# One division step for the first two head pairs: the softmax sums of layer 1 taken together

## The chip, the cores and the metric

The kernel runs as one launch on one core of a Trainium2 chip. The metric is the device time of that launch in microseconds (us); a kernel's time is the median over several executions. Before the change it is 3047.86 us, the median of 3 runs from 3046.55 to 3050.51.

## The reference, cut to what matters

Eight images of 384 channels and 32 x 32 pixels, that is 1024 tokens of 384 channels, pass through two layers in fp32. Layer 0 (group norm, attention with a relative bias, a residual) isn't touched. Layer 1 does the following, and the change is in its attention, whose softmax is divided only after the product with v:

```
t = to_tokens(x)
t = t + attention(layer_norm(t))       # 6 heads of 64; q and k normalised over each head
t = t + feed_forward(layer_norm(t))    # images 0 to 4 only; the reference leaves the output
                                       # of the last three images at zero there
attention:
    attn = softmax(einsum('bhnd,bhmd->bhnm', q, k) * scale, axis=-1)
    out  = einsum('bhnm,bhmd->bhnd', attn, v)
    return out @ proj_w.T + proj_b
```

## The kernel before, in words

Layer 1 works on one image after the other. The six heads of an image are three **pairs** (0, 1 and 2): the two heads of a pair, j = 0 and 1, lie in the two halves of the 128 partitions. The 1024 queries are two halves (h, 512 each), and the 1024 keys are eight groups of 128, taken two at a time (m2 = 0 to 3). A **unit** is one (pair, h, m2), so an image has 24 units, numbered 0 to 23 here: pair 0 is units 0 to 7, pair 1 is 8 to 15, pair 2 is 16 to 23.

The loop over units is written out by hand, and every engine gets its instructions in the order of the text:

- `scores` (L1322) makes the scores s of a unit on TensorE in two PSUM tiles; ScalarE takes the exponential of them into two SBUF tiles e (L1333). VectorE adds the e tiles of a half into running sums t (L1345 for the first two, L1348 after). At m2 = 3 it adds the two halves of t into one half of a tile `folded[pair, j]`, named f in the profile (L1353).
- `weigh` (L1371) multiplies e with v into the PSUM tile o. It runs two units behind `scores` (LAG = 2), between the scores of its step and those of the next one. When a half is finished, ScalarE and VectorE bring o into `oT` (L1380, L1381).
- `divide` is called once for each pair, when the last unit of the pair has been weighed: for pair 0 in step 9 of the loop, for pair 1 in step 17, for pair 2 after the loop. Four matmuls with a column of ones (L1394, tile sum) give the sums over partitions for (j, h), each in its own group of 32 PSUM partitions. ScalarE copies them out (L1399, tile sr), SyncE's queue sends them to DRAM (L1408, sd) and fetches them again spread over 128 partitions (L1409, inv). VectorE takes the reciprocal (L1412), SyncE's queue writes it to DRAM (L1414, rd) and fetches it twice broadcast over 64 partitions (L1417, rb). VectorE multiplies `oT[:, pair]` by rb (L1419).

The waiting parts of `divide` are put off with `later.after(n, work)`: the work is placed n steps of the loop later, so that its instructions stand behind those of the units in between.

Buffers set part of the order. PSUM has four tiles of two banks (`mm2`), shared by s, o, sum and everything else. SBUF has a pool of 16 tiles of 128 x 1024 (`wtile`), which e, t, f, sr and the squares of the next image share. rb has one buffer. At step 3 of an image the next image is loaded, and its sums and squares (L1109, L1122, L1128, L1132) are placed at steps 13, 14, 15, 19 and 20.

After the loop, images 0 to 4 run the output projection (`project_out`, L1435) and the feed-forward; images 5 and 6 run the next image's q, k and v, with the projection put into the next image's loop; image 7 finishes with pair 2's division and the projection.

```
if done and done[0][1:] == (NH - 1, MT // 2 - 1):
    divide(b, oT, done[0][0])
later.step()
```

Of the kernel before, what the change touches and what calls it, by code (L numbers as in the profile page):

```python
# [19 lines left out]
F32 = mybir.dt.float32  # L20
# [7 lines left out]
P = 128  # L28
QP = P // 2
B, C, IH, IW = 8, 384, 32, 32  # L30
N = IH * IW
KC = C // P
MT = N // P
HALF = 512
NH = N // HALF
# [16 lines left out]
H1, D1 = 6, 64  # L52
NP1 = H1 // 2
# [43 lines left out]
class _Shared:  # L97
# [13 lines left out]
    def mm2(self, name):  # L111
        return self.ps.tile([P, NH, HALF], F32, tag="p", name=name)
# [918 lines left out]
def _layer1(tc, ins, x1, out, shared, start, before=None, check=None):  # L1031
# [3 lines left out]
    nc = tc.nc  # L1035
    with ExitStack() as ctx:

        def pool(name, bufs):
            return ctx.enter_context(tc.tile_pool(name=name, bufs=bufs, reuse_waits="tile"))
# [5 lines left out]
        small = pool("b_small", 2)  # L1045
        dram = ctx.enter_context(tc.tile_pool(name="b_dram", bufs=2, space=DRAM))
        later = _Later()
        mm2 = shared.mm2
        rsqrt, ones = shared.rsqrt, shared.ones

        def wtile(name, shape=(P, N)):
            return work.tile(list(shape), F32, tag="w", name=name)

        def flat2(t):
            return t.rearrange("p h q -> p (h q)")
# [253 lines left out]
        acc, total, folded = {}, {}, {}  # L1309
# [75 lines left out]
            for finish in weigh(b, oT, *done) or ():  # L1385
                finish()

        def divide(b, oT, pair, steps=(2, 2)):


            pst = mm2(f"sum{b}_{pair}")
            for h in range(NH):
                for j in range(2):
                    nc.tensor.matmul(  # L1394
                        pst[ts(2 * j + h, 32), 0], ones[:, 0:32], folded[pair, j][:, ts(h, HALF)],
                        start=True, stop=True,
                    )
            rows = wtile(f"sr{b}_{pair}", (P, HALF))
            nc.scalar.copy(rows, pst[:, 0])  # L1399
            sd = dram.tile([4, HALF], F32, tag="sd", name=f"sd{b}_{pair}")  # L1400
            rd = dram.tile([2, N], F32, tag="rd", name=f"rd{b}_{pair}")
            inv = small.tile([P, 2 * N // P], F32, tag="inv", name=f"inv{b}_{pair}")

            def spread(t):
                return t.rearrange("a q -> (a q)").rearrange("(p c) -> p c", p=P)

            with nc.allow_non_contiguous_dma(reason="sums"):
                nc.sync.dma_start(sd, rows[0:P:32])  # L1408
                nc.sync.dma_start(inv, spread(sd))  # L1409

            def invert():
                nc.vector.reciprocal(inv, inv)  # L1412
                with nc.allow_non_contiguous_dma(reason="sums"):
                    nc.sync.dma_start(spread(rd), inv)  # L1414
                rb = room.tile([P, N], F32, tag="rb", name=f"rb{b}_{pair}")
                for j in range(2):
                    nc.sync.dma_start(rb[ts(j, D1)], rd[j].partition_broadcast(D1))  # L1417
                later.after(
                    steps[1], lambda: nc.vector.tensor_mul(oT[:, pair], oT[:, pair], rb)  # L1419
                )  # L1420

            later.after(steps[0], invert)

# [187 lines left out]
        def head_rows(b):  # L1611
            return dram.tile([NP1, 8, HALF], F32, tag="hs", name=f"hd{b}")
# [49 lines left out]
        for b in range(B):  # L1662


            assert B // NG == 1
            ffn, more = b < NG, b + 1 < B
            oT = None
            if b == 1 and check is not None:
                for i, stage in enumerate(check(wtile)):
                    later.after(2 * i + 5, stage)  # L1670
            held = []
            for i, u in enumerate(units):
                done = held.pop(0) if len(held) == LAG else None
                held.append(
                    (u, scores(b, qk, kc, u, lambda: weigh(b, oT, *done) if done else None))
                )
                if done and done[0][1:] == (NH - 1, MT // 2 - 1):
                    divide(b, oT, done[0][0])
                later.step()
                if i == 3:  # L1680
                    if behind is not None:
                        behind()
                        behind = None
                    oT = wide.tile([P, KC, N], F32, tag="o", name=f"oT{b}")
                    ahead = load(b + 1) if more else None
                    if more:
                        *ahead_sums, stages = fold(f"a{b + 1}", ahead)
                        for at, stage in zip((13, 14, 15, 19, 20), stages):
                            later.after(at - i, stage)
            if not more:  # L1690
                for done in held:
                    weigh_last(b, oT, done)
                divide(b, oT, NP1 - 1)
                later.finish()
                project_out(b, oT, xt, lambda m: store(b, xt, m))
                break
            if not ffn:

                def last(i, b=b, oT=oT, held=held):
                    weigh_last(b, oT, held[i])  # L1700
                    if i == 1:
                        divide(b, oT, NP1 - 1, (2, 4))

                nqk, nkc = attention_inputs(
                    b + 1, ahead, [lambda: last(0), lambda: last(1)], ahead_sums
                )
                behind = lambda b=b, oT=oT, xt=xt: project_out(
                    b, oT, xt, lambda m: store(b, xt, m)
                )
            else:  # L1710
                nqk, sq, d, nkc = {}, {}, head_rows(b + 1), kc_tile(b + 1)

                def project(pair, s, step=True, middle=None):
                    return project_qk(b + 1, pair, s, ahead, nqk, sq, step, middle)

                def normalise(pair, *steps):
                    normalise_qk(b + 1, pair, nqk, d, nkc, steps)

                for i in range(2):
                    project_v(b + 1, ahead, i)  # L1720
                    weigh_last(b, oT, held[i])
                divide(b, oT, NP1 - 1, (1, 1))
                project_v(b + 1, ahead, 2)
                fsq, fc = [], []
                project_out(b, oT, xt, lambda m: fsq.append(square(f"f{b}", xt, m)), later.step)
                two = wtile(f"two{b}")
                nc.vector.tensor_add(two, xt[:, 0], xt[:, 1])
                nc.vector.tensor_add(fsq[0], fsq[0], fsq[1])
                project(
                    0, 0,  # L1730
                    middle=lambda: fc.append(
                        token_sums(f"f{b}", (xt[:, KC - 1], two), (fsq[KC - 1], fsq[0]))
                    ),
                )
                un, begin, normal = layer_norm(b, xt, fc[0])
                tk = token_sums(f"a{b + 1}", *ahead_sums)
                project(0, 1)
                take = project(1, 0, step=False)
                begin()
                take()  # L1740
                later.step()
                head_sums(b + 1, 0, sq, d)
                take = project(1, 1, step=False)
                normal()
                take()

                def between_1(m):
                    if m == 2:
                        normalise(0, 5, 2)
                    elif m == 4:  # L1750
                        head_sums(b + 1, 1, sq, d)
                        normalise(1, 5, 3)

                y1, top = feed_forward_1(b, un, between_1)
                project(2, 0)
                quant_scale(top)
                supply = Supply(b, y1, top)
                supply.gelu(0)
                supply.gelu(1)
                supply.split(0)  # L1760
                project(2, 1, step=False)()
                supply.split(1)
                supply.gelu(2)
                project_v(b + 1, ahead, MT // 2 - 1, copy=nc.scalar.copy)

                def between_2(k):
                    if k == 0:
                        head_sums(b + 1, 2, sq, d)
                        normalise(2, 6, 3)
                    elif k == 4:  # L1770
                        token_stats(f"a{b + 1}", tk)
                    elif k > 4 and (k - 5) % 2 == 0:
                        scale_v(tk, (k - 5) // 2)

                feed_forward_2(b, supply, between_2, xt)
            xt, qk, kc = ahead, nqk, nkc
# [74 lines left out]
```

## Time and profile before

| | us |
|---|---|
| median of 3 runs | 3047.86 |
| the profiled execution's own time | 3046.46 |
| its span (first to last instruction) | 3044.7 |
| TensorE busy in the span | 3018.3 |
| VectorE busy | 1772.1 |
| ScalarE busy | 1401.9 |
| GpSimd busy | 465.1 |

The span is what the profile's times are counted in. The profiled execution took 1.76 us more than its span, and 1.40 us less than the median of the runs. A matmul with fp32 operands shows as two records. Ends of matmuls are modelled in the profile and overlap the next matmul's start, so distances on TensorE are read from start to start. "PEld" is TensorE's weight load, "SPq" is SyncE's queue, which issues the DMAs.

### The profile page before, as it was taken

The numbers are of one execution on the slowest core, as the hardware profiler recorded it, in microseconds if no ns is written. First come the engines' busy times: TensorE is split into PE (matmuls) and PEld (weight loads), VectorE is DVE, ScalarE is ACT, GpSimd is POOL, SyncE is SP. The second block draws the span as 40 slices with busy tenths as digits, with TensorE's granted clock in tenths as the row PEclk, the third lists the DMA queues.
The fourth block names the chain that finished last, engine by engine and source line by source line (L and its number), as shares of the span: only waits on it lengthen the run. The fifth ranks groups of instructions, "written<-read, shape, count | busy, mean of one in ns | idle before, by whom it ended". The sixth has DMA issues, their size and how long they took to land.

```text
span 3044.7 us, 45670 instructions
## 1 busy us (share of the span) xinstructions
PE 3018.3 (99%) x18914; PEld 1598.8 (53%) x18914; DVE 1772.1 (58%) x1768; ACT 1401.9 (46%) x1768; POOL 465.1 (15%) x315
## 2 busy tenths in 40 slices
PE   8999999999999999999999999999999999999998
PEld 3455546455554645444545645645645646645453
DVE  3746647373655727355565765765755755754555
ACT  2634526253443616244463553553553544654544
POOL 0111102021110202123202202202202202211110
PEclk9999999999999999999999999999999999999999
DMA  7412020211212020121401101101101101102011
GB/s 178 119 25 83 19 82 23 72 30 26 76 22 79 23 83 19 37 87 51 120 23 37 50 16 37 50 23 30 50 23 30 50 22 30 55 12 72 16 51 44
DMA packets 102769, 150.49 MB, mean 49 GB/s; under 512 B 62260, under 2 KB 65828, under 8 KB 101784
## 3 DMA queue, kind: packets, MB, share of 16 engines
q1 hardware_dynamic: 99688, 147.41, 17.2%
q8 instruction: 152, 2.49, 0.3%
q14 instruction: 65, 0.53, 0.1%
q10 hardware_dynamic: 2864, 0.05, 0.1%
HBM read 111.05 MB, written 27.32 MB: 45 GB/s over the span
## 4 chain that ended last, share of the span: by engine, by line
PE 96%; DMA 1%; DVE 1%; SPq 1%; issue 0%; ACT 0%; ACTq 0%; DVEq 0%
PE s L521 14%; PE o L552 14%; PE s L1322 11%; PE o L1371 11%; PE pq L1178 8%; PE pq L467 8%; PE y2p L1575 6%; PE y1p L1524 5%; PE pp L616 4%; PE pv L1259 4%; PE pp L1435 4%; PE pv L495 4%; PE sum L1394 1%; PE hs L1207 1%; SPq L391 1%; DMA wide<-table 0%
## 5 line engine op out<-in xcount | busy, mean ns | idle before, releaser
L536 ACT ACTIVATE e<-e 128x1024 f32<-128x1024 f32 x512 | 535.0, 1057 | 441.7 <-DVE e L532 421.8
L532 DVE TENSOR_TENSOR e<-s,grow 128x1024 f32<-128x1024 f32 x512 | 601.4, 1219 | 190.3 <-PE s L521 189.7
L521 PE MATMUL s<-qk 48*64 48x512 f32 x4096 | 611.1, 591 | 3.2 <-DVE e L532 3.1
L552 PE MATMUL o<-e,v 64*64 64x512 f32 x4096 | 607.4, 589 | 1.4 <-DVE e L532 1.4
L1333 ACT ACTIVATE e<-s,kc 128x512 f32<-128x512 f32 x768 | 463.4, 693 | 181.8 <-PE s L1322 165.2
L1322 PE MATMUL s<-qk,qk 64*64 64x512 f32 x3072 | 398.7, 592 | 1.3 <-DVE oT L1381 1.2
L1371 PE MATMUL o<-e,v 64*64 64x512 f32 x3072 | 395.6, 591 | 0.0
L521 PEld LDWEIGHTS s<-qk 48*64 48x64 f32 x4096 | 237.2, 132 | 228.5 <-issue 76.0
L552 PEld LDWEIGHTS o<-e,v 64*64 64x64 f32 x4096 | 259.7, 133 | 178.9 <-issue 72.0
L1348 DVE TENSOR_TENSOR t<-t,e 128x1024 f32<-128x1024 f32 x192 | 231.0, 1222 | 65.6 <-ACT e L1333 65.6
L1178 PE MATMUL pq<-bx,wqkv 128*128 128x512 f32 x576 | 255.4, 597 | 0.7 <-ACT tra L1150 0.7
L467 PE MATMUL pq<-xn,w 128*128 128x512 f32 x576 | 251.8, 598 | 0.0
L1322 PEld LDWEIGHTS s<-qk,qk 64*64 64x64 f32 x3072 | 148.9, 133 | 195.5 <-issue 116.3
L581 POOL TENSOR_TENSOR inv<-sums,over 128x16 f32<-128x16 f32 x32 | 92.7, 2898 | 1008.7 <-DMA sums<-sd 850.0
L1371 PEld LDWEIGHTS o<-e,v 64*64 64x64 f32 x3072 | 148.3, 133 | 180.5 <-issue 142.5
L467 PEld LDWEIGHTS pq<-xn,w 128*128 128x128 f32 x576 | 109.8, 192 | 142.7 <-issue 140.0
L1178 PEld LDWEIGHTS pq<-bx,wqkv 128*128 128x128 f32 x576 | 107.7, 190 | 145.0 <-issue 141.3
L1345 DVE TENSOR_TENSOR t<-e,e 128x1024 f32<-128x1024 f32 x96 | 114.2, 1224 | 58.5 <-ACT e L1333 58.3
L1511 DVE TENSOR_REDUCE parts<-y 128x1 f32<-128x1024 f32 x75 | 90.0, 1217 | 93.8 <-ACT y L1508 93.3
L1228 POOL TENSOR_TENSOR hc<-hc,rsqrt 128x32 f32<-128x32 f32 x24 | 140.1, 5836 | 2.0
L1194 ACT ACTIVATE qsq<-pq 128x1024 f32<-128x1024 f32 x48 | 49.1, 1024 | 194.1 <-DVE qk L1188 105.5
L477 DVE TENSOR_SCALAR qk<-pq,bqk 128x1024 f32<-128x1024 f32 x24 | 30.8, 1284 | 177.5 <-PE pq L467 177.5
(161 smaller groups left out, 3032.1 us busy)
## 6 DMA issues: line engine op xcount, KB each, us to landing
rb<-rd SPq DMA_DIRECT2D x112, 256.0 KB
xn<-in_x_dram SPq DMA_DIRECT2D x24, 512.0 KB
res<-in_x_dram SPq DMA_DIRECT2D x24, 512.0 KB
x<-res SPq DMA_DIRECT2D x24, 512.0 KB
bx<-x SPq DMA_DIRECT2D x8, 1536.0 KB
rq<-hi SPq DMA_DIRECT2D x48, 256.0 KB
out_dram<-bx SPq DMA_DIRECT2D x24, 512.0 KB
wide<-table SPq DMA_DIRECT2D x80, 114.2 KB
```

Source lines behind the costliest of these rows:

```text
L467: nc.tensor.matmul(pq[:, h], wqk[:, k, s, 2 * pair : 2 * pair + 2, :].rearrange("p h d -> p (h d)"), xn[:, k, ts(h, HALF)], start=(k == 0) ...
L521: nc.tensor.matmul(s[j][ts(c, QP), i], qk[pair][rows, 1, ts(4 * m2 + 2 * i + c, QP)], qk[pair][rows, 0, ts(h, HALF)], start=True, stop=True,)
L532: nc.vector.tensor_add(e.rearrange("p (i q) -> p i q", i=2), s[j], bass.AP(near.tensor, near.offset, [near.ap[0], [-QROWS * IW, 2], [1, HA ...
L536: nc.scalar.activation(e, e, AF.Exp)
L552: nc.tensor.matmul(po[ts(j, S0), r], v[keys, 2 * m2 + i, 2 * pair + j, :], es[j][keys, ts(i, HALF)], start=(m2 == 0 and i == 0), stop=(m2 ...
L1178: nc.tensor.matmul(pq[:, h], wqkv[:, k, s * C + pair * P : s * C + (pair + 1) * P], xt[:, k, ts(h, HALF)], start=(k == 0), stop=(k == KC - 1),
L1322: nc.tensor.matmul(s[j][ts(c, QP), i], qk[pair, 1][rows, ts(4 * m2 + 2 * i + c, QP)], qk[pair, 0][rows, ts(h, HALF)], start=True, stop=True,)
L1333: nc.scalar.activation(e[:, ts(i, HALF)], s[j][:, i], AF.Exp, scale=kc[:, pair, j, m : m + 1])
L1348: nc.vector.tensor_add(total[j], total[j], e)
L1371: nc.tensor.matmul(po[ts(j, D1), r], v[keys, 2 * m2 + i, at : at + D1], es[j][keys, ts(i, HALF)], start=(m2 == 0 and i == 0), stop=(m2 == ...
L1524: nc.tensor.matmul(py[m][:, h], w1[:, k, ts(m, P)], un[k][i][:, ts(h, HALF)], start=(k == 0 and i == 0), stop=(k == KC - 1 and i == 1),)
L1575: nc.tensor.matmul(py[m][:, h], w2[:, k, ts(m, P)], supply.parts[k][i][:, ts(h, HALF)], start=(k == 0 and i == 0), stop=(k == FC - 1 and i ...
```

## The change

`divide` takes a list of pairs. It is called once for the pairs 0 and 1, in step 17, where it stood for pair 1 before; pair 2 has a call of its own as before. For two pairs the sums are eight matmuls into both banks of one PSUM tile, the copy takes 128 x 1024 elements, sd, inv and rd hold twice as much, and there is one reciprocal. Each pair still has its own rb and multiplication: `use(0)` fetches rb for pair 0; two steps later pair 0 is multiplied and `use(1)` fetches rb for pair 1, which is multiplied two steps after that. So pair 0 is multiplied in step 20 (it was step 12) and pair 1 in step 22 (it was step 20). The tiles f of pair 0, first written in step 3, are held up to step 17 (they were free after step 9). Per image there are one copy, one reciprocal and three DMAs fewer.

```diff
-        def divide(b, oT, pair, steps=(2, 2)):
-            pst = mm2(f"sum{b}_{pair}")
-            for h in range(NH):
-                for j in range(2):
-                    nc.tensor.matmul(
-                        pst[ts(2 * j + h, 32), 0], ones[:, 0:32], folded[pair, j][:, ts(h, HALF)],
-                        start=True, stop=True,
-                    )
-            rows = wtile(f"sr{b}_{pair}", (P, HALF))
-            nc.scalar.copy(rows, pst[:, 0])
-            sd = dram.tile([4, HALF], F32, tag="sd", name=f"sd{b}_{pair}")
-            rd = dram.tile([2, N], F32, tag="rd", name=f"rd{b}_{pair}")
-            inv = small.tile([P, 2 * N // P], F32, tag="inv", name=f"inv{b}_{pair}")
+        def divide(b, oT, pairs, steps=(2, 2)):
+            n = len(pairs)
+            name = f"{b}_{pairs[0]}"
+            pst = mm2(f"sum{name}")
+            for i, pair in enumerate(pairs):
+                for h in range(NH):
+                    for j in range(2):
+                        nc.tensor.matmul(
+                            pst[ts(2 * j + h, 32), i], ones[:, 0:32],
+                            folded[pair, j][:, ts(h, HALF)], start=True, stop=True,
+                        )
+            rows = wtile(f"sr{name}", (P, n * HALF))
+            nc.scalar.copy(rows, flat2(pst[:, 0:n]))
+            sd = dram.tile([4, n * HALF], F32, tag=f"sd{n}", name=f"sd{name}")
+            rd = dram.tile([4, n * HALF], F32, tag=f"rd{n}", name=f"rd{name}")
+            inv = small.tile([P, n * 2 * N // P], F32, tag=f"inv{n}", name=f"inv{name}")
...
                     nc.sync.dma_start(spread(rd), inv)
+                use(0)
+
+            def use(i):
+                pair = pairs[i]
                 rb = room.tile([P, N], F32, tag="rb", name=f"rb{b}_{pair}")
                 for j in range(2):
-                    nc.sync.dma_start(rb[ts(j, D1)], rd[j].partition_broadcast(D1))
-                later.after(
-                    steps[1], lambda: nc.vector.tensor_mul(oT[:, pair], oT[:, pair], rb)
-                )
+                    nc.sync.dma_start(
+                        rb[ts(j, D1)].rearrange("p (h q) -> p h q", h=NH),
+                        bass.AP(
+                            rd.tensor, rd.offset + (2 * j * n + i) * HALF,
+                            [[0, D1], [n * HALF, NH], [1, HALF]],
+                        ),
+                    )
+
+                def multiply():
+                    nc.vector.tensor_mul(oT[:, pair], oT[:, pair], rb)
+                    if i + 1 < n:
+                        use(i + 1)
+
+                later.after(steps[1], multiply)
...
-                if done and done[0][1:] == (NH - 1, MT // 2 - 1):
-                    divide(b, oT, done[0][0])
+                if done and done[0] == (NP1 - 2, NH - 1, MT // 2 - 1):
+                    divide(b, oT, range(NP1 - 1))
```

The three other calls pass `[NP1 - 1]` for `NP1 - 1`.

More of the change, by code (lines that the diff above doesn't have):

```diff
@@ L1692, in _layer1 @@
                     weigh_last(b, oT, done)
-                divide(b, oT, NP1 - 1)
+                divide(b, oT, [NP1 - 1])
                 later.finish()
@@ L1701, in last @@
                     if i == 1:
-                        divide(b, oT, NP1 - 1, (2, 4))
+                        divide(b, oT, [NP1 - 1], (2, 4))
                 nqk, nkc = attention_inputs(
@@ L1721, in _layer1 @@
                     weigh_last(b, oT, held[i])
-                divide(b, oT, NP1 - 1, (1, 1))
+                divide(b, oT, [NP1 - 1], (1, 1))
                 project_v(b + 1, ahead, 2)
```

## The prediction

> **What bounds the kernel now.** I read the page's busy times first, then its chain of work, then TensorE's instructions in order of time around one of the steps that the change touches (image 2, pair 1), then VectorE's.
>
> ```profile
> PE 3018.3 (99%) x18914; PEld 1598.8 (53%) x18914; DVE 1772.1 (58%) x1768; ACT 1401.9 (46%) x1768; POOL 465.1 (15%) x315
> ...
> PE 96%; DMA 1%; DVE 1%; SPq 1%; issue 0%; ACT 0%; ACTq 0%; DVEq 0%
> ```
>
> TensorE is busy 99% of the span and is 96% of the chain. Only what shortens TensorE's stream, or makes it wait, can count. What VectorE, ScalarE and the DMAs save is worth nothing by itself, and what they lose is free as long as TensorE doesn't wait for it. The timeline of TensorE (start, length, engine, line):
>
> ```profile
> 2004.66 2.08 PE L1322 MATMUL s<-qk,qk 64*64 64x512 f32 x16
> 2006.37 2.08 PE L1371 MATMUL o<-e,v 64*64 64x512 f32 x16
> 2008.38 1.07 PE L1394 MATMUL sum<-f,ones 128*32 128x512 f32 x8
> 2009.38 1.95 PE L1322 MATMUL s<-qk,qk 64*64 64x512 f32 x16
> 2011.15 1.91 PE L1371 MATMUL o<-e,v 64*64 64x512 f32 x16
> 2012.88 0.61 PE L1322 MATMUL s<-qk,qk 64*64 64x512 f32 x4
> ```
>
> In the undisturbed loop a group of 16 records starts every 1.717 us (half of a unit's 3.434). The sum stands between two units. From 2004.66 to 2012.88 are 8.22 us; the four groups alone would take 6.87. So the interruption costs **1.35 us**: 1.00 for the sum itself (2008.38 to 2009.38), 0.29 of delay before it (2.01 instead of 1.72), 0.06 after it. Read in the same way, by counting records between starts, the 16 interruptions of the pairs 0 and 1 cost 1.24 to 1.45 us each, 21.5 us in all, 1.35 on average. No other group in that stretch of the loop is late: with the sums left out, TensorE is at its pace.
>
> [...]the sums are 128*32 between 64*64 groups and lose 0.24 to 0.45 us beside their own 1.00, and their eight records, 0.6 us each, fit in 1.00 us.[...] From issue to last landing, sd takes 1.70 us with 8 KB, and hd, of the same kind with 16 KB, takes 1.76[...].[...]
>
> **The change part by part**, for one image.
>
> *The interruption at pair 0's place goes* (step 9). This takes away 1.00 for the sum and 0.24 to 0.45 for going there and back.
>
> *The sum at pair 1's place grows by eight records* (step 17). The nearest evidence of their price is another sum with ones, whose passes follow each other:
>
> ```profile
> 2066.39 0.60 PE L1145 MATMUL tsf<-two,ones 128*32 128x512 f32 x2
> ...
> 2066.82 0.60 PE L1145 MATMUL tsf<-two,ones 128*32 128x512 f32 x2
> ```
>
> A pass over the same columns of the array takes 0.43 us (2066.39 to 2066.82). Four column groups run beside each other, so eight records are two passes, 0.86, and 1.00 with 0.14 at the ends. Eight more are two more passes: +0.86, and I take 0.88. Bounds: 0.86 below, a full 1.00 above. The merged interruption then costs 1.35 + 0.88 = 2.23, and eight of them 17.8. **Gain: 21.5 - 17.8 = 3.7 us.** With a remaining interruption of the cheap kind (1.24 + 0.86) it is 4.7; with the dear kind and a full second sum (1.45 + 1.00) it is 1.9.
>
> *ScalarE* copies 1024 elements once (about 1.05 us, from the 1.02 of the 128x1024 square of pq at L1194) for two copies of 0.59. It waits about 1 us in each unit for scores, and the next scores can't be ready before the eight added records are through: hidden. Without that slack the copy would cost 0.46 an image.
>
> *The DMAs.* One sd, inv and rd for two, three issues fewer; SyncE's queue has nothing else to issue until pair 2's sd, so the second rb, which waits there for the multiplication of pair 0 to free the one buffer, holds nobody. inv, sd and rd of the new size are those of hc, hd and hi (16 KB): 1.65, 1.76 and 1.41 us against 1.60, 1.70 and 1.40 now. rb comes in runs of 2 KB, as rq does: median 4.26 us against 3.89.
>
> *VectorE*, where the multiplications move. Steps 20 to 22 of image 2 in VectorE's timeline:
>
> ```profile
> 2021.59 1.23 DVE L1419 TENSOR_TENSOR oT<-oT,rb 128x1024 f32<-128x1024 f32 x1 [0.45 <-DMA rb<-rd]
> 2022.99 2.38 DVE L1345 TENSOR_TENSOR t<-e,e 128x1024 f32<-128x1024 f32 x2 [0.17 <-ACT e L1333]
> 2025.29 0.68 DVE L1381 TENSOR_TENSOR oT<-o,oT 128x512 f32<-128x512 f32 x1
> 2026.42 2.39 DVE L1348 TENSOR_TENSOR t<-t,e 128x1024 f32<-128x1024 f32 x2 [0.45 <-ACT e L1333]
> ```
>
> Pair 0's multiplication will stand where pair 1's stands (first line); it already waits 0.45 us for rb. The longer copy (+0.46) and the longer sd and inv (+0.11) are hidden: the reciprocal at step 18 doesn't wait for its DMA now, because it stands behind VectorE's adds; inv lands some 0.9 us earlier. What is left is rb's 0.37 and rd's 0.01: about 0.4 us later. Behind it stand the adds of step 21 (0.17 of slack), then L1381, which frees o's PSUM tile; the scores of step 23 take that tile, at 2026.61. L1381 ends at 2025.97, so 0.64 us are free; some 0.25 to 0.4 of them go. TensorE isn't held, but by only about 0.3 us. Pair 1's multiplication at step 22 comes after adds that end at 2028.8; its rb, issued after the first multiplication, lands near 2028.4. It adds 1.23 us to VectorE there, in front of step 23's adds and f. Only image 7 feels that: its last sum follows directly on f, whose adds had 1.05 us to spare. Cost 0.2 us, once; below nothing it can't be, since nothing is taken away there.
>
> *SBUF.* The order of instructions shows one new tight reuse in images 0 to 6: the second e tile of unit 16 takes the tile of t (pair 1, second half, j = 0), so that exponential must wait for the first f of step 15. That f ends at 2003.56 in image 2 and the exponential starts at 2004.54: 0.98 us apart, cost nothing. If that went, ScalarE's 1 us of slack would be used next.
>
> *The end* (pair 2's chain to the last projection) keeps its instructions; only its rb is written in another way in the text, with the same 64 x 1024 transfer.
>
> **The sum.** -3.7 + 0.2 = -3.5 us. Against the profiled execution's own time, 3046.46 (span 3044.7 and 1.76 around it), this gives 3042.96. That execution lies 1.40 below the median of the runs, so the median should come to 3047.86 - 3.5 = **3044.4**.
>
> **The rivals.** A difference of 0.2% (6.1 us) is about what a measurement of this kernel can tell from no change.
>
> *A: the saved interruption, as worked out.* 3043.4 to 3046.2 by the bounds; 3044.4. For it: start times on an engine that is 99% busy. Chance 0.66.
>
> *B: the added passes and the drain eat the gain.* If the eight records cost more than a second full sum, or the merged interruption drains for longer, the kernel is where it was: 3046 to 3049. Against it: the 0.43 us passes. Chance 0.10.
>
> *C: VectorE's multiplication at step 20 becomes the bound (slower).* If rb lands more than about 0.3 us later than I reckon, L1381 frees o's tile too late and the scores of step 23 wait, microsecond for microsecond, in the seven images that also add squares at step 20. At 1.7 us later the loss is (1.7 - 0.3) x 7 = 9.8, which with the gain is +6.3: slower by 0.2%. At 2 us: +8.4, 3056. For it: rb and rq vary from 3.4 to 6.1 us[...]. Against it: nothing else is loaded in those steps. Chance 0.12, with a mild form of it (3045 to 3049) inside A and B.
>
> *D: the drain goes almost wholly.* If a merged interruption cost its four passes and ends alone (1.86), the gain would be 21.5 - 14.9 = 6.6 us, with image 7's 0.2 off 3041.5. Against it: each of the 16 places shows at least 0.24 beside the sum. Chance 0.12, the spread of the medians included.
>
> **How the numbers follow.** The likeliest case gives the time, 3044.4. The range takes in A, B up to 1.1 us over the old median and D with 1 us of spread: 3040.5 to 3049.0, leaving out C and the edges. Faster by over 0.2% (under 3041.8): D and the edge of A, 0.16. Slower by over 0.2% (over 3053.9): C, 0.12. Between: 0.72.
>
> **What would show it.** Right: the sum has 16 records and about 1.86 us from its start to the next scores, eight times instead of sixteen in the loop; the group before step 10's scores is at its 1.72 pace; L1345 and L1381 of steps 20 and 21 are later by about 0.4 us against TensorE. Wrong: scores of step 23 that wait for L1381; exponentials of unit 16 that wait for VectorE; a second pair of passes over 1.0 us.

## The result, and the profile after

The changed kernel takes **3041.89 us** (median of 20 runs, 3040.6 to 3045.25) beside 3047.55 us for the kernel before (20 runs, 3045.82 to 3050.52). The ratio is 0.9983, with a 95% interval from 0.9977 to 0.9989: 5.2 us less (3.4 to 7.0). Two more sets of runs of the same kernel gave 0.9984 [0.9977, 0.9992] and 0.9982 [0.9974, 0.9990]. The forecast was 3.5 us less and a time of 3044.4. The profiled execution took 3043.66 us, its span 3041.8, against 3046.46 and 3044.7 before.

The busy times and the chain of work on the page of the changed kernel:

```profile
PE 3017.7 (99%) x18914; PEld 1610.8 (53%) x18914; DVE 1769.1 (58%) x1760; ACT 1402.7 (46%) x1760; POOL 465.0 (15%) x315
...
PE 93%; DMA 3%; DVE 3%; ACT 1%; SPq 1%; issue 0%; POOL 0%; ACTq 0%; DVEq 0%; POOLq 0%
```

VectorE and ScalarE have eight instructions less each (one reciprocal, one copy per image), and TensorE is still the bound. Its busy time fell by 0.6 us while the span fell by 2.9. But in two traces of the kernel before it is 3018.3 and 3022.0 us, so busy times can't say where the gain lies.

The timeline of TensorE around the merged sum of image 2 (start, length, engine, line):

```profile
2004.10 0.59 PE L1371 MATMUL o<-e,v 64*64 64x512 f32 x1
2004.33 0.60 PE L1322 MATMUL s<-qk,qk 64*64 64x512 f32 x3
2004.53 2.13 PE L1371 MATMUL o<-e,v 64*64 64x512 f32 x15
2006.58 1.92 PE L1398 MATMUL sum<-f,ones 128*32 128x512 f32 x16
2008.44 1.95 PE L1322 MATMUL s<-qk,qk 64*64 64x512 f32 x16
2010.20 1.90 PE L1371 MATMUL o<-e,v 64*64 64x512 f32 x16
```

The sum has 16 records and lasts from 2006.58 to 2008.44, **1.86 us**, the predicted figure. They start in four sets of four, within 0.02 us in a set, and the sets begin 0.43 to 0.45 us apart (2006.58, 2007.04, 2007.47, 2007.89). The first two lines of the view show what the prediction didn't see: the first o record of a group starts 0.23 us before the last three s records of the group ahead of it. The groups of s and o also consist of four sets of four records 0.43 us apart, but here three records of each set start 0.67 us after the first one (in the o group: one at 2004.10, three from 2004.76 to 2004.78), while in the first set behind the sum all four start within 0.02 us (2008.44 to 2008.46). I call this distance the **lag**. The trace shows it in the start times; where it comes from it doesn't show.

Where the 5.2 us lie I read from marks: the ninth scores record of every unit. Summed over the eight images from unit 0 to unit 23, the **loops** take 668.59, 667.99, 668.37 and 669.19 us in the four traces that run the loop of before (mean 668.5), and 665.50, 664.55, 664.94 and 664.90 in the four that run the changed one (mean 665.0). That is **3.6 us** less; the forecast was 3.5. The other part is at the **end**: from the start of the last addition bx (L1440, now L1458) to the end of the span the kernel before takes 9.06 us, the changed one 7.13. The waits of SyncE's own queue in that stretch (engine, line, waited for: us in total, times, longest), first before, then after:

```profile
SPq L1446 <- DVE bx L1440: 11.0, 3, 8.2
SPq L1796 <- SPq L1796: 4.8, 2, 2.9
SPq L1847 <- PEq L1847: 0.6, 2, 0.5
```

```profile
SPq L1464 <- DVE bx L1458: 10.8, 3, 8.0
SPq L1814 <- SPq L1814: 2.9, 1, 2.9
SPq L1865 <- PEq L1865: 0.6, 2, 0.5
```

L1796 (L1814) is the branch around the code for inputs out of range, which isn't taken up here. Behind it SyncE goes through eight short waits. Before, it is held there twice for nothing but itself, 2.9 us and 1.9 us; after, only the 2.9. **The 1.9 us are gone, and no line of the change is near.**

Everything outside the loops and the end took 2.1 us longer in this trace of the changed kernel than in that of before, so the two spans differ by only 2.9. I don't credit this to the change: among four traces of one and the same loop, that part differs by up to 3.0 us before and 3.7 after.

### The profile page after: what moved, and what is told of

The parts are those of the page before. It is cut to its first block, busy times and chain, and to the rows that moved or that the text cites. A ratio compares the mean times of both kernels' runs of the same rounds, so it can differ in the third digit from the quotient of the medians.

```text
span 3041.8 us, 45673 instructions
## 1 busy us (share of the span) xinstructions
PE 3017.7 (99%) x18914; PEld 1610.8 (53%) x18914; DVE 1769.1 (58%) x1760; ACT 1402.7 (46%) x1760; POOL 465.0 (15%) x315
## 4 chain that ended last, share of the span: by engine, by line
PE 93%; DMA 3%; DVE 3%; ACT 1%; SPq 1%; issue 0%; POOL 0%; ACTq 0%; DVEq 0%; POOLq 0%
PE s L521 15%; PE o L552 14%; PE s L1322 11%; PE o L1371 11%; PE pq L467 8%; PE pq L1178 6%; PE y2p L1593 6%; PE pp L616 4%; PE pv L1259 4%; PE y1p L1542 4%; PE pp L1453 4%; PE pv L495 4%; PE sum L1398 1%; DMA wide<-table 1%; PE hs L1207 1%; DVE lun L1494 1%
## 5 line engine op out<-in xcount | busy, mean ns | idle before, releaser
L552 PE MATMUL o<-e,v 64*64 64x512 f32 x4096 | 607.5, 589 | 0.0
L1322 PE MATMUL s<-qk,qk 64*64 64x512 f32 x3072 | 418.6, 592 | 1.1 <-DVE oT L1381 0.9
L1371 PE MATMUL o<-e,v 64*64 64x512 f32 x3072 | 414.9, 590 | 0.0
L552 PEld LDWEIGHTS o<-e,v 64*64 64x64 f32 x4096 | 259.4, 133 | 178.5 <-issue 71.1
L1371 PEld LDWEIGHTS o<-e,v 64*64 64x64 f32 x3072 | 158.8, 133 | 169.9 <-issue 142.6
```

The lines of the kernel that those rows point to most:

```text
L552: nc.tensor.matmul(po[ts(j, S0), r], v[keys, 2 * m2 + i, 2 * pair + j, :], es[j][keys, ts(i, HALF)], start=(m2 == 0 and i == 0), stop=(m2 ...
L1322: nc.tensor.matmul(s[j][ts(c, QP), i], qk[pair, 1][rows, ts(4 * m2 + 2 * i + c, QP)], qk[pair, 0][rows, ts(h, HALF)], start=True, stop=True,)
L1371: nc.tensor.matmul(po[ts(j, D1), r], v[keys, 2 * m2 + i, at : at + D1], es[j][keys, ts(i, HALF)], start=(m2 == 0 and i == 0), stop=(m2 == ...
```

## The experiments

In three sets, each on one chip; "before" is the kernel before on the same chip. Loops and ends are from one trace of each; those called "before" are from the trace of the kernel before that the prediction used.

### First set: parts of the change (before: 3046.15)

**after_again**, the changed kernel once more.

> The changed kernel once more, unchanged, for a second trace. Theory 1 (the gain is TensorE's, from interruptions of the unit loop that are no longer made): the eight unit loops are together 3.1 us shorter than in the trace of before, as in the first trace of the changed kernel, within 0.2 us; time about 3042. Theory 2 (of the 5.2 us between the medians, what exceeds 3.1 is no effect of the change, but waits on DMAs in the feed-forward and after the last store that differ from execution to execution): outside the unit loops this trace differs from the first one of the changed kernel by 1 us or more. Theory 3 (the rest, about 2 us, comes from three DMAs, a copy and a reciprocal fewer per image, or from multiplications that moved): outside the loops the two traces of the changed kernel agree, and both are shorter there than before.

Measured: 3040.94 us, loops 4.0 us under the trace of before, end 7.19. All loops but two agree within 0.02 us with those of the other trace of this kernel: image 1 (0.7 us shorter) and image 7 (0.2 shorter). So a few tenths in a loop can be read, except in image 1.

**chains_apart**: only the sums are taken together; each pair keeps a copy, sd, inv, reciprocal and rd of its own.

```diff
-            rows = wtile(f"sr{name}", (P, n * HALF))
-            nc.scalar.copy(rows, flat2(pst[:, 0:n]))
+            for i, pair in enumerate(pairs):
+                chain(b, oT, [pair], pst[:, i], (steps[0], steps[1] + 2 * i))
```

> The opposite half: the eight sum matmuls stay together in step 17, but each pair has its own copy, sd, inv, reciprocal and rd again (multiplications in steps 20 and 22 as in the changed kernel). Theory 1: as the changed kernel, 3042, within 1 us. Theory 3: about 2 us slower than the changed kernel, 3044.

Measured: 3040.88 us, ratio 0.9982 [0.9975, 0.9988]; loops 3.9 us less, end 7.20. The one copy, one reciprocal and three DMAs saved are worth nothing that shows.

**split_sums**: the opposite. Pair 0's sums go back to step 9 with a copy of their own into half of a shared tile; all behind the copies stays as in the changed kernel.

```diff
+                if done and done[0] == (0, NH - 1, MT // 2 - 1):
+                    both = wtile(f"sr{b}_0", (P, 2 * HALF))
+                    collect(b, 0, both[:, 0:HALF])
                 if done and done[0] == (1, NH - 1, MT // 2 - 1):
-                    divide(b, oT, range(NP1 - 1))
+                    collect(b, 1, both[:, HALF : 2 * HALF])
+                    divide(b, oT, range(NP1 - 1), rows=both)
```

> The sums of pair 0 go back to their own place in step 9, with a copy of their own into half of a shared tile; the DMAs, the reciprocal and the multiplications stay merged and late, as in the changed kernel. Theory 1: TensorE is interrupted 16 times again, so the time is that of before, 3047.5, within 1 us. Theory 3 (the merged chain brings part of the gain): about 2 us faster than before, 3045.5; if the chain brings all of it, 3042.

Measured: 3044.61 us, 0.9998 [0.9989, 1.0006]; loops 0.3 us less than before, end 7.12. With both interruptions back, the gain in the loops is gone, though the chain is merged and late. The end is short here too, so it isn't the sums that shorten it.

**no_pair0**: the kernel before without pair 0's division: it leaves out that pair's sums, chain and multiplication.

```diff
-                if done and done[0][1:] == (NH - 1, MT // 2 - 1):
-                    divide(b, oT, done[0][0])
+                if done and done[0] == (1, NH - 1, MT // 2 - 1):
+                    divide(b, oT, 1)
```

> The kernel before, without any division of pair 0: no sums, chain or multiplication for it (the part of the computation that is left out). Measures what one interruption of the loop costs. Theory 1: the eight interruptions at pair 0's place cost 1.16 to 1.57 us each in the traces, 11.3 in all, so 3047.5 - 11.3 = 3036.2; the counting by starts gave 10.9, 3036.6. Theory 3: the chain that is gone too makes it about 2 us faster still, 3034.

Measured: 3036.9 us, 0.9970 [0.9959, 0.9982]; loops 9.8 us less, end 7.17. This is what leaving out pair 0's division brings in the loops; the merge brings 3.6 of these 9.8 us.

### Second set: the price of the passes, and the rival with the late multiplication (before: 3047.57)

**before_again**, the kernel before once more.

> The kernel before once more, unchanged: the zero of the measurement, and a second trace of before. Ratio 1.000 within 0.0008. Theory 2 (the 1 to 2 us by which the medians differ beyond the unit loops, and the end after the last loop that is 2 us longer in the first trace of before, are spread of executions): the end after the last loop comes down from 34.7 us towards the 32.6 to 34.4 of the other kernels, and the stretches between the loops move by 0.5 us or more. Theory 4 (before is really slower outside the loops): the end stays at 34.7 within 0.2 us. In the loops both expect 668.6 us for the eight together, within 0.3, but for image 1, where two waits of TensorE for L1381 (1.2 us) may come out otherwise.

Measured: 3048.19 us, 1.0000 [0.9992, 1.0009]; loops 0.6 us less, through image 1 (0.7 less); end 9.01. The long end belongs to this kernel and isn't an accident of one trace.

**sums_thrice**: the changed kernel with pair 0's four sum matmuls issued twice.

```diff
-            for i, pair in enumerate(pairs):
+            order = list(enumerate(pairs))
+            for i, pair in order[:1] + order if n > 1 else order:
```

> The changed kernel with the four sum matmuls of pair 0 issued twice (eight records more in the merged place, 24 in all). Measures the price of the added passes. If passes follow each other at 0.43 us, the sum takes 1.85 + 0.86 = 2.71 us from its start to the next scores and the kernel 8 x 0.86 = 6.9 us more than the changed kernel: 3048.5 to 3049. If each group of eight costs a full 1.00 with its ends, 8.0 more. If the interruption hides passes (a rival under which the added sums are nearly free), under 3 more.

Measured: 3050.25 us, 1.0009 [1.0000, 1.0017]; loops 4.2 us over before. TensorE's timeline of this kernel, image 2:

```profile
2006.24 2.78 PE L1399 MATMUL sum<-f,ones 128*32 128x512 f32 x24
2008.96 1.95 PE L1322 MATMUL s<-qk,qk 64*64 64x512 f32 x16
```

From the sum to the next scores are 2.72 us with 24 records, 1.86 with 16, 1.00 with 8: each two passes cost **0.86**. The loops grew by 8 x 0.86 = 6.9 us through that. They are 7.8 over the changed kernel's mean: the images 6 and 7 lost another 0.6 and 1.2 us ahead of their last unit, while image 1, which loses 0.8 there on average in the changed kernel, lost nothing. In 6 and 7 the scores waited for L1381, which stands behind the multiplication for pair 0 (1.3 us in two waits): a first, mild sight of the slower rival.

**one_hop_more**: the changed kernel with one more 16 KB copy in DRAM (re from rd, 1.98 us from issue to landing) ahead of rb.

```diff
                     nc.sync.dma_start(spread(rd), inv)
+                if n > 1:
+                    nc.sync.dma_start(src, rd)     # src: a second DRAM tile, re
                 use(0)
```

> The changed kernel with one more DRAM-to-DRAM copy of 16 KB between rd and rb for the pairs 0 and 1, so that both rb land about 1.7 us later. Tests the margin of VectorE's multiplication at step 20. In the trace of the changed kernel L1381 of step 21 ends about 0.6 us before the scores of step 23 that take its PSUM tile. If that margin is what counts, 1.7 us of delay leave 1.0 to 1.2 us of waiting in each of seven images: 7 to 8 us slower than the changed kernel, about 3049, with waits of the scores for L1381 in the trace. If the delay is hidden all the same, 3041 to 3042.

Measured: 3058.67 us, 1.0035 [1.0021, 1.0048]; loops 11.5 us over before, about 15 over the changed kernel. VectorE's timeline and one line of TensorE's, image 2:

```profile
2024.35 1.23 DVE L1437 TENSOR_TENSOR oT<-oT,rb 128x1024 f32<-128x1024 f32 x1 [2.27 <-DMA rb<-re]
2025.50 2.35 DVE L1345 TENSOR_TENSOR t<-e,e 128x1024 f32<-128x1024 f32 x2
2027.77 0.68 DVE L1381 TENSOR_TENSOR oT<-o,oT 128x512 f32<-128x512 f32 x1
```

```profile
2028.51 2.04 PE L1322 MATMUL s<-qk,qk 64*64 64x512 f32 x16 [0.84 <-DVE oT L1381]
```

The multiplication waits 2.27 us for rb and starts at 2024.35, the adds behind it start at 2025.50, L1381 behind them at 2027.77, and the scores of step 23 wait for L1381's tile. TensorE's waits over the whole of layer 1, first in the changed kernel, then in this one:

```profile
PE s L1322 <- DVE oT L1381: 0.9, 1, 0.9
```

```profile
PE s L1322 <- DVE oT L1381: 13.3, 8, 2.2
```

This is the slower rival, with its mechanism and place: eight waits, 12.4 us more in all, and all eight images lost, not only the seven that the prediction named. The loss is about twice the 7 to 8 us expected. Image 2, shown here, is the mildest, with 1.1 us ahead of its last unit by the marks; the others lost 1.3 to 3.0. The multiplication came 1.6 to 2.8 us later after the sums than in the changed kernel (1.3 in image 1), not 1.7 throughout.

### Third set: the end of the program (before: 3047.65)

In every kernel of the first two sets but before_again the end took 7.1 to 7.2 us, whatever its sums. What they share is that SyncE's program has another length than in the kernel before. In the changed kernel (and in split_sums and sums_thrice) it has 24 DMAs fewer in the main part, 24 fewer in the skipped branch and 8 semaphore instructions more, so that the code behind the branch stands 40 instructions earlier; in one_hop_more it stands 36 earlier, in no_pair0 96 earlier, in chains_apart 28 later. In the gap of the kernel before (3041.1 to 3042.9 us) one transfer is under way, by the DMA queues (queue, kind: packets, MB, share):

```profile
q14 instruction: 1, 0.01, 1.2%
```

It is a packet of 8192 bytes, from a queue of the kind that the profile calls instruction; it starts at 3041.44 and takes 0.34 us. In all traces, with the gap or without, such a packet starts 5.7 to 6.1 us after the last bx does; in the changed kernel it runs from 3040.43 to 3040.92, and SyncE goes on through it, an instruction every 0.05 to 0.07 us. With the gap one packet more follows, in the kernel before at 3043.57. What SyncE waits for in the gap the traces don't show. Three of the four kernels of this set move the code behind the branch and change nothing that is executed, by loads inside the branch, which this input skips (30 loads more bring 10 semaphore instructions with them, 118 also 10):

```diff
+        for _ in range(31):                          # 119 in before_period
             nc.sync.dma_start(gmat, ins["gmat"].rearrange("(k p) c -> p k c", p=P))
```

**before_padded**, the kernel before with that.

> The kernel before, with 31 more loads of gmat inside the branch that is skipped for this input (L1797 and what it calls): no instruction that is executed differs. In SP's program the code behind the branch moves back by 40 instructions; in the changed kernel it moves forward by 40. In both traces of before, SP's eight last waits at L1796 are cut after the third by a gap of 1.9 us, which no other kernel of this study shows. Theory ([...]its place in the program decides whether it falls there): the gap is gone, last bx start to the end of the span 7.1 us in place of 9.06, SP waits once for itself at L1796 in place of twice, unit loops as in before (within 0.7), time lower by 1.9 us: 3045.7 beside 3047.6, ratio 0.9994. Rival (the shorter end comes of the merged sums, fewer stores or transfers under way at the end): end 9.0, ratio 1.000.

**after_padded**, the changed kernel with that.

> The changed kernel with the same 31 loads of gmat inside the skipped branch, which brings the code behind the branch back to the place that it has in the kernel before (the two SP programs then have the same number of instructions). Theory of the program's place: the gap comes back after the third of SP's waits, last bx start to end 9.06 us in place of 7.1, two waits of SP for itself, unit loops as in the changed kernel (3.1 to 4.0 below before), time 1.9 us above the changed kernel: 3043.8 beside before's 3047.6, ratio 0.9988. Rival (the end is shorter because of the merge): end 7.1, ratio 0.9983, as the changed kernel beside it.

**before_period**, the kernel before with 119 loads.

> The kernel before with 119 loads of gmat in the skipped branch: the code behind the branch moves back by 128 SP instructions. An instruction packet in the trace's queue q14 is 0.53 MB over 65, 8.2 KB[...]. Theory of the program's place with a period of 128: the gap is again after the third wait, end 9.06, ratio 1.000. [...]if any pad removes the gap: end 7.1, ratio 0.9994.

**after_beside**, the changed kernel unpadded.

> The changed kernel once more, to stand beside the padded ones on one chip: end 7.1 us, unit loops 3.1 to 4.0 us below before, ratio 0.9983. If the theory of the program's place holds, its distance to the padded kernel before is the gain of the loops alone: 3.3 us, 0.11 per cent.

| | time, us | ratio [95%] | loops, us | end, us | SyncE's waits for itself |
|---|---|---|---|---|---|
| before | 3047.65 | | 668.6 | 9.06 | 2 |
| before_padded | 3045.28 | 0.9993 [0.9986, 0.9999] | 668.4 | 7.11 | 1 |
| before_period | 3047.34 | 0.9999 [0.9990, 1.0007] | 669.2 | 9.03 | 2 |
| after_beside | 3042.23 | 0.9982 [0.9974, 0.9990] | 664.9 | 7.14 | 1 |
| after_padded | 3044.63 | 0.9988 [0.9982, 0.9995] | 664.9 | 9.07 | 2 |

SyncE's waits for itself, first in before_padded, then in after_padded:

```profile
SPq L1797 <- SPq L1797: 2.8, 1, 2.8
```

```profile
SPq L1815 <- SPq L1815: 4.8, 2, 2.8
```

The same pad takes the gap from one kernel and gives it to the other, after the third of the eight waits, as in the kernel before; a shift of 128 instructions leaves it where it was. The 128 was a guess of mine; no trace shows how many instructions a packet holds. **Where SyncE's code lies decides over 1.9 us, and the merge only happened to move it.** The medians form a square: the pad takes 2.4 us from the one and adds 2.4 to the other, and the merge itself gains 3.0 us beside each (3047.65 to 3044.63, 3045.28 to 3042.23).

The stop right behind the branch is there in every kernel of the table: 2.8 to 2.9 us, the longest of SyncE's waits for itself.

## Why the prediction was right, and where it was not

**The bound and the price of the passes: right.** 0.86 us for each two passes, 1.86 for the sum, as worked out from the other sum with ones. sums_thrice confirms the price. chains_apart and split_sums show that the merged sums, and nothing behind them, make the gain in the loops.

**The sum of the interruptions: mis-sized by 0.6 us, and by luck other terms made up for it.** By the marks, which take in what a start-to-start reading of single groups leaves out, the interruptions of before cost 22.6 us (the prediction: 21.5) and the eight merged ones 19.5 (17.8). The gain is 3.1, not 3.7. The term that fails is in "1.35 + 0.88 = 2.23": the time beside the passes, 0.24 to 0.45 us before. The prediction calls it the drain and carries it over as it was. The traces show how long it is, not what TensorE does in it, and its length goes with the lag. I measure that by the **spread** of a group, the time from its first record start to its last: 1.31 us where the four records of each set start together, 1.97 with the lag of 0.67 above. At the sums, from the mark before to the mark after, less 3.434 for a unit:

| place | spread of the group | interruption |
|---|---|---|
| before, pair 0, images 0, 6, 7 | 1.31 | 1.16 |
| before, pair 0, images 1 to 5 | 1.84 to 1.85 | 1.57 |
| before, pair 1, image 2 | 1.49 | 1.34 |
| before, pair 1, image 7 | 1.31 | 1.16 |
| after, image 7 | 1.31 | 2.02 |
| after, images 0 and 6 | 1.50 | 2.21 |
| after, image 2 | 1.97 | 2.42 |

In the kernel before another 0.08 to 0.09 us follow in the unit after the sum, at pair 0's place and in image 7. So without lag (image 7) two interruptions of 1.25 became one of 2.02: 0.48 us saved, about the 0.46 forecast for an image. With lag (image 2), 1.64 and 1.35 became 2.42 and 0.18, the latter a growth of the lag at unit 15 that the marks show: 0.39 saved. The lag is paid in either kernel: before, 0.40 at step 9 and 0.11 at step 17; after, 0.18 at unit 15 and 0.41 at step 17. In the kernel before the lag also ended at the interruption of step 9 (image 2: a spread of 1.85 us in the last group ahead of it, 1.36 in the first o group behind it, 1.31 in the next); in the changed kernel it goes on to step 17 (1.85, then 1.79, at last 1.97). So taking the first interruption out only puts that part of the cost off. no_pair0 shows this by itself. In its image 4, where the sums of step 9 are gone, 0.24 us appear at unit 15 and the interruption at step 17 costs 1.57 in place of 1.34 (at a spread of 2.02): of the 1.64 us taken out, 1.18 are won. The reading fits all places of the table; no run took the lag itself away.

What made up for it: in image 1 the scores waited for L1381, by 0.4 to 1.8 us in the four traces with the loop of before and by 0.2 to 0.9 in the four with the changed one, and the loop there is 1.0 shorter on average, with a wide spread; image 3 lost 0.28 between its units 1 and 2 in all four traces of the changed kernel, for a cause I did not find; and the 0.2 us for image 7 were seen in one trace of four. Together: -0.40 x 5 in the images 0, 2, 4, 5 and 6, -1.0, -0.13 and -0.42 in 1, 3 and 7, that is -3.6. That this comes so near to the forecast is the luck of image 1.

**The edits costed at nothing: right.** ScalarE's copy took 1.01 us for 1024 elements, and ScalarE still idles ahead of it and behind it:

```profile
2008.68 1.01 ACT L1403 COPY sr<-sum 128x1024 f32<-128x1024 f32 x1 [0.74 <-PE sum L1398]
2010.49 0.69 ACT L1333 ACTIVATE e<-s,kc 128x512 f32<-128x512 f32 x1 [0.80 <-PE s L1322]
```

VectorE's timeline where the multiplications now stand:

```profile
2020.87 1.23 DVE L1434 TENSOR_TENSOR oT<-oT,rb 128x1024 f32<-128x1024 f32 x1 [0.61 <-DMA rb<-rd]
2022.03 2.38 DVE L1345 TENSOR_TENSOR t<-e,e 128x1024 f32<-128x1024 f32 x2
2024.33 0.68 DVE L1381 TENSOR_TENSOR oT<-o,oT 128x512 f32<-128x512 f32 x1
...
2027.77 1.22 DVE L1434 TENSOR_TENSOR oT<-oT,rb 128x1024 f32<-128x1024 f32 x1
```

Pair 0's multiplication waits 0.61 us for rb (0.45 before). Against TensorE, which is 0.95 us earlier here, it is 0.2 us later, not 0.4: rb landed after 3.96 us in the median, not 4.26, so rq was the wrong row to take. L1381 follows in time. The exponentials of unit 16 wait for the scores (1.01 us), not for VectorE, so the new reuse of an SBUF tile costs nothing here.

**The rivals.** *C* is real but lay further off: one_hop_more shows it eat the gain three times over at 2 us of delay; the changed kernel has 0.2 us of it, in image 7 of one trace. *B* did not happen, but for the 0.6 us above. *D* named 3041.5, near the result, but not for its reason: the merged interruption costs 2.0 to 2.4 us, not 1.86.

**The step that failed** is "The end ... keeps its instructions". It does, and it still became 1.9 us shorter, because 40 instructions ahead of it went. The prediction asked of moved and removed instructions what waits for them, but not where they leave the code behind a branch. Of the 2.5 us by which the forecast missed, this is 1.9 (by the trace) to 2.4 (by the medians). after_padded, the change without this accident, takes 3044.63 us; the forecast was 3044.4.

## What to carry to other kernels

When one engine is busy all the time, count the interruptions of its stream, price the passes that stay, and compare the spread of the groups ahead of an interruption and behind it. Here it fell from 1.85 to 1.31 us at step 9, and in image 4 of no_pair0 only 1.18 of the 1.64 us taken out were won. Where a multiplication moves nearer to a buffer's release, ask what slack stands behind it: 0.64 us in image 2 here, and a further copy of 2 us cost twelve in waits. For differences of about 0.1%, compare the end of the program and its waits before crediting the change; a pad in a branch that isn't taken told the place of the code from the work here, 1.9 us at the end from 3.6 in the loops.

## What I had not expected of the hardware

- The place of a program's code alone was worth 1.9 us: a stop among SyncE's last eight waits (3041.1 to 3042.9 in the kernel before), which is there again after a shift of 128 instructions (end 9.03 us) and not after shifts of 28, 36, 40 or 96 (ends of 7.1 to 7.2).
- The last projection (12 records from the last rb's multiplication on) takes 5.43 us in some executions and 7.12 in others, of either kernel. The chain of before and that of before_again:

```profile
3030.14 5.43 PE pp L1435 x12
```

```profile
3029.33 7.12 PE pp L1435 x12
```

  Its first weight loads in before_again start 0.86 us apart (3030.34, 3031.20, 3032.05), those from 3032.83 on 0.43, as in the first trace of before from 3030.68 on. The mean granted clock from 3025 to 3040 us is 0.87 in before_again and 0.96 in that trace. The wait ahead of the projection doesn't tell the two kinds of execution apart: 2.4 us ahead of the 5.43 in the kernel before, 2.5 ahead of the 7.12, and 2.3 ahead of 7.13 in after_padded. What decides it the traces don't show.
- The lag: groups of 16 records had spreads from 1.31 to 2.02 us at one and the same pace of 1.717 us per group. Where groups of s and o followed each other, a lag that stayed about the same cost nothing: the units 11 to 13 of image 2 in the changed kernel, with spreads of 1.79 to 1.84, take 3.43 us each, as they do at 1.31 in the kernel before.
